# A two-layer graph kernel on one core: no product for the padded key, moments from every fourth row tile, U1's projections in more banks, spare transposes at the start

## The chip, the core and the metric

The kernel runs on one core of one Trainium2 chip. The metric is the device time of one execution in microseconds (us). The kernel before took 2207.8 us (median of three runs, 2207.56 to 2210.33).

## What is computed

`x` is 3327 x 256, `adj` is 3327 x 3327, sparse with its diagonal set, all float32. Two layers follow each other, each on a layer norm and relu of `x`, and each result is added to `x`. Cut to what matters here:

```python
# layer 0, on h = relu(layernorm(x))
R = (adj + eye) / rowsum(adj + eye)
Z, Xf, Xa = 0, h, h
for n in range(2):
    q, k = Xa @ W1.T @ W2.T, Xa @ W3.T          # 64 wide
    probs = softmax(q @ k.T)                    # 3327 x 3327
    A = probs with each row cut to its top entries summing to 0.9, renormalised
    Xf, Xa = R @ Xf, A @ Xa
    Z = Z + Xf @ U1[n].T + Xa @ U2[n].T
x = x + layernorm(h + Z) * ln_g + ln_b

# layer 1: 4-head neighbour attention on relu(layernorm(x)), then elu, added to x
```

## The kernel before, in words

**Tiles.** The 3327 rows are 26 tiles of 128; the last has 127 real rows, so tile arrays are one column longer (3328) than the real data. Work goes row tile by row tile, twice (two steps), and then through the neighbour attention of layer 1.

**Stages.** (1) The start: 26 loads of `x` (L1830 in `load_x`), mean and deviation on VectorE and GpSimd (`deviations`), relu on ScalarE (L1169), two transposes per tile on TensorE (L1174) copied to `c` (L1177), then one product per tile with the combined weights `wqk` that gives keys and queries together (L1182), copied to a ring of three `kq` buffers (L1188) and spread from there by GpSimd (L1191, L1192) and a DMA (L1195). (2) `project_u`: each tile of `h` times both U1 matrices (two products of 128 x 512, L1218). Half of the result goes to `main` by ScalarE (L1221), the other half to `c` by VectorE (L1222). (3) Two steps of 26 rows each. A row's `search` makes its logits in two parts (L882, into two `pl` tiles of two banks each), exponentials (L896), counts over the whole row at two or three guessed thresholds (L933), candidate windows on VectorE (L988, L993), a sort and choice, and four pieces that zero what falls below the threshold (L1043). `attention` then transposes the row (26 transposes, L1056) and multiplies (26 products of 128 x 256, L1068, in the bank `acca`). `full` multiplies a row tile of `adj` with the source (26 products, L1100, in the bank `accf`). (4) Neighbour attention in four blocks (L1644, L1660, L1674).

**The padded key.** Logits for the last 255 keys come in two halves of 128 and 127 columns, one from each half of the 128 partitions. For the 3328th column, which is no key, a product of two constant tiles `none` (L890) writes -1000 into the logits, so that its exponential is 0.

**The moments.** The first threshold is guessed from mean and variance of each row's logits, which follow from the sum of the keys and of their outer products. `moments` takes them from a sample of key tiles: a transpose of the tile's `kq` (L771), a copy to one of two `kk` buffers (L775), a product of 128 x 65 (L780), and additions to `gk` (L792). `keys_summed` puts it for every second tile, 13 per step, in step 0 in the banks `acca` and `accf`, in step 1 in `px`. `stats` (L807 and after) makes the rows' figures of it.

**What sets the order.** The order is made when the program is built: `Plan` (class at L470) is a planner that runs at build time. Every piece of work is put with an engine, an assumed length, a rank, its needs, and the buffers that it takes and gives back. The planner walks through the assumed time, gives each free engine the ready piece with the lowest rank, and writes the instructions in that order. On the chip each engine works through its own list in that order and waits where an operand or a buffer is not ready. The buffers in PSUM are `pl` (two of two banks each), `acca` and `accf` (one bank each) and `px` (two of one bank each). In the start `px` serves the key products, U1's projections and the statistics.

`project_u` is planned at rank -1.9 (TensorE), its copies at -2.6, a row's logits and exponentials at 2.5 below the row's number.

Of the kernel before, what the change touches and what calls it, by code (L numbers as in the profile page):

```python
# [469 lines left out]
class Plan:  # L470
# [26 lines left out]
    def order(self):  # L497
        free, events = dict(self.free), []
        now = dict.fromkeys(self.LAG, 0.0)
        ready = {e: [] for e in self.LAG}  # L500

        def finish(p, end):

            heapq.heappush(events, (end, p["k"], p, "own"))
            heapq.heappush(events, (end + p["lag"], p["k"], p, ""))
            for b in p["give"]:
                heapq.heappush(events, (end + p["lag"], p["k"], p, b))

        for k, p in enumerate(self.pieces):
            p["k"], p["left"], p["from"] = k, len(p["needs"]), 0.0  # L510
            if not p["left"]:
                ready[p["engine"]].append(p)
        out, clock, holds = [], 0.0, []
        while len(out) < len(self.pieces):
            while events and events[0][0] <= clock:
                _, _, p, what = heapq.heappop(events)
                if what == "end":

                    held = sum(max(0.0, min(z, clock) - max(a, p["at"])) for a, z in holds[-12:])
                    end = p["at"] + p["length"] + held  # L520
                    if end > clock + 1e-6:
                        now[p["engine"]] = end
                        heapq.heappush(events, (end, p["k"], p, "end"))
                    else:
                        finish(p, clock)
                    continue
                if what not in ("", "own"):
                    free[what] += 1
                    continue
                for q in p["then"]:  # L530
                    if (q["engine"] == p["engine"]) == (what == "own"):
                        q["left"] -= 1
                        if not q["left"]:
                            ready[q["engine"]].append(q)
            for e, queue in ready.items():
                if now[e] > clock or not queue:
                    continue
                can = [p for p in queue if all(free[b] >= p["take"].count(b) for b in p["take"])]
                if not can:
                    continue  # L540
                p = min(can, key=lambda q: q["rank"])
                queue.remove(p)
                for b in p["take"]:
                    free[b] -= 1
                p["at"] = clock
                now[e] = clock + p["length"]
                if p["hold"]:
                    holds.append((clock, clock + p["hold"]))
                if e == "POOL":
                    heapq.heappush(events, (now[e], p["k"], p, "end"))  # L550
                else:
                    finish(p, now[e])
                out.append(p)
            times = [t for e, t in now.items() if t > clock and ready[e]] + ([events[0][0]] if events else [])
            later = [t for t in times if t > clock]
            if not later:
                if len(out) < len(self.pieces):
                    raise RuntimeError("the plan stands still")
                break
            clock = min(later)  # L560
        self.end = max(now.values())
        return out
# [8 lines left out]
def fast(  # L571
# [59 lines left out]
    with ExitStack() as l0:  # L631
# [16 lines left out]
        kt = wpool.tile([P, 3 * 512 + P], F32, name="kt")  # L648
        qq = wpool.tile([P, NT, P], F32, name="qq")


        none = wpool.tile([P, P + 2], F32, name="none")
        GP.memset(none, 0.0)
        GP.memset(none[DA : DA + 32, :P], 1.0)
        GP.memset(none[DA : DA + 32, P:], -1.0e3)
        kks = [wpool.tile([P, P + 2], F32, name=f"kk{k}") for k in range(2)]
        for kk in kks:
            GP.memset(kk[:, :: P + 1], 1.0)
# [103 lines left out]
        def moments(t, kq, ps_k, ps_g):  # L762


            r, p = side(t), min(P, N - t * P)
            half = slice(r * DA, r * DA + DA)
            held = {}

            def turn():
                held["ps"] = ps_k()  # L770
                T.transpose(held["ps"][:, :P], kq(), ident)  # L771

            def copy():
                kk = held["kk"] = kks[t // 2 % 2]
                S.copy(kk[:, 1 : P + 1], held["ps"][:, :P])  # L775

            def product():
                kk = held["kk"]
                ps = held["ps"] = ps_g()
                T.matmul(  # L780
                    ps[:, : DA + 1], kk[:p, 1 : P + 1], kk[:p, r * (DA + 1) : (r + 1) * (DA + 1)], start=True, stop=True
                )

            def gather():
                for to, src in (
                    (gk[half, :DA], held["ps"][half, 1 - r : DA + 1 - r]),
                    (gk[half, DA : DA + 1], held["ps"][half, DA * r : DA * r + 1]),
                ):
                    if t in (0, 4):
                        V.tensor_copy(to, src)  # L790
                    else:
                        V.tensor_add(to, to, src)  # L792

            return turn, copy, product, gather
# [59 lines left out]
        class Row:  # L854
# [18 lines left out]
            def logits(self, k):  # L873

                if k == 0:
                    self.open()
                pl = ps_l.tile([P, 2, 512], F32, name="pl")
                w = 512 if k < 3 else P
                for r in range(2):
                    m = min(w, N - 1024 * k - w * r)  # L880
                    half = slice(r * DA, r * DA + DA)
                    T.matmul(  # L882
                        pl[:, r, :m],
                        qq[half, self.i, :],
                        kt[half, 512 * k : 512 * k + m],
                        start=True,
                        stop=True,
                    )
                    if m < w:
                        T.matmul(pl[:, r, m:w], none[half, :P], none[half, P : P + w - m], start=True, stop=True)  # L890
                self.pl[k] = pl[:, :, :w]

            def exps(self, k):
                pl = self.pl.pop(k)
                w = pl.shape[2]
                S.activation(  # L896
                    self.e[:, 1024 * k : 1024 * k + 2 * w].rearrange("p (r w) -> p r w", r=2),
                    pl,
                    AF.Exp,
                    accum_out=(self.p0, self.p1, self.p2, self.p3)[k],  # L900
# [94 lines left out]
            def free(self):  # L995

                GP.tensor_scalar(self.room, self.h0, self.h1, self.b, ALU.add, ALU.subtract)
                GP.tensor_scalar(self.rec, self.s, self.h0, self.h1, ALU.subtract, ALU.subtract)

            def sort(self):  # L1000

# [159 lines left out]
        def prepare(t, measured):  # L1161
# [32 lines left out]
            def double():  # L1194
# [7 lines left out]
            a = plan.put("ACT", 0.3, r, share, needs=[a], take=["kq"], give=["px"])  # L1202
            k = plan.put("POOL", 0.7, r, keys, needs=[a])
            q = plan.put("SP", 0.2, r, double, needs=[a])
            g = t % 2 == 0 and keys_summed(
                t, lambda: held["kq"], lambda: ps_a.tile([P, P], F32, name="acca"),
                lambda: ps_a.tile([P, DA + 1], F32, name="accf"), r, [a], ("acca", "accf"), [],
            ) or None
# [3 lines left out]
        def project_u(t, rank):  # L1212
            held = {}

            def product():
                ps = held["ps"] = ps_x.tile([P, 2 * D], F32, name="px")
                for k in range(2):
                    T.matmul(ps, c[:, t, k * P : (k + 1) * P], u1[:, k, :], start=(k == 0), stop=(k == 1))  # L1218

            a = plan.put("PE", 1.75, rank, product, needs=[turned_h[t], uloads], take=["px"])  # L1220
            b = plan.put("ACT", 0.37, -2.6, lambda: S.copy(main[:, t, :D], held["ps"][:, :D]), needs=[a])  # L1221
            e = plan.put("DVE", 0.43, -2.6, lambda: V.tensor_copy(c[:, t, :], held["ps"][:, D:]), needs=[a])  # L1222
            plan.put("SP", 0.0, -2.6, lambda: None, needs=[b, e], give=["px"], lag=0.0)
            return b, e

        def finish1(row, done, rank):
# [59 lines left out]
            if direct:  # L1286
# [2 lines left out]
                    plan.put("POOL", 0.4, r, queries, needs=[a, drawn[0]]),  # L1289
                ]  # L1290
            kq.append(plan.put("SP", 0.3, r, spread, needs=[a, drawn[0] if direct else None]))
            g = t % 2 == 0 and keys_summed(
                t, lambda: held["kq"], lambda: ps_x.tile([P, P], F32, name="px"),
                lambda: ps_x.tile([P, DA + 1], F32, name="px"), r, [a, guessed[0]], ("px", "px"), [],
            ) or None
# [123 lines left out]
        def search(row, rank, keys, stats_of, fresh):  # L1419
# [4 lines left out]
            for g in range(2):  # L1424

                def logits(g=g):
# [1 line left out]
                    row.logits(2 * g + 1)  # L1428

                a = plan.put(  # L1430
                    "PE", 2.1 - 0.7 * g, rank - 2.5, logits, needs=[keys, fresh, a], take=["pl", "pl"] + ["e", "sc"] * (1 - g)
                )
                for k in (2 * g, 2 * g + 1):
                    got.append(
# [394 lines left out]
        def load_x(t):  # L1829
            nc.sync.dma_start(rhs[0][:, t, :], x[t * P : (t + 1) * P, :])  # L1830

        uloads = []
        weighed = weights()
        loads = [plan.put("SP", 0.58, -200.0 + t, load_x, t) for t in range(NT)]
# [8 lines left out]
        for n in range(STEPS):  # L1843
            base = 30.0 * n
            scaled = plan.put(
                "DVE", 0.2, base - 50.0,
                lambda: V.tensor_scalar(gk[:, : DA + 1], gk[:, : DA + 1], 1.0 / (NT // 2 * P), None, ALU.mult), needs=[sums],
            )
            cuts = (0, 3, NT // 2, NT)
            of = {}  # L1850
# [121 lines left out]
```

## Time and profile before

| What | Value |
|---|---|
| Median of three runs | 2207.8 us |
| The profiled execution | 2208.77 us |
| Its span | 2207.0 us |
| TensorE busy | 2169.5 us, 98% |
| VectorE busy | 1614.3 us, 73% |
| ScalarE busy | 1443.2 us, 65% |
| GpSimd busy | 932.8 us, 42% |
| First instruction of TensorE | 5.96 us |
| First logits (L882) | 46.9 us |
| First transposed row piece (L1056) | 105.1 us |
| Last logits (L882) | 1637 us |

The profile is one execution. "PE" is TensorE's matmuls and "PEld" its weight loads; DVE is VectorE, ACT ScalarE, POOL GpSimd, SP the engine that issues most DMAs. A line of the groups names the source line, the engine, the operation, what is written and read, the shape and the number of records. A float32 product leaves two records of TensorE, a transpose one. [...] records overlap, and the pace is read from the distance of starts. A line of the timeline merges a run of equal instructions: start, length, what, number of records, and in brackets an idle time before it with what ended it.

### The profile page before, as it was taken

The page shows a single profiled execution, that of the slowest core. Times are in us where ns is not written, and L with a number is a line of the kernel's source. Part 1 is how long each engine was busy: PE and PEld are TensorE (multiplying, and loading weights), DVE is VectorE, ACT ScalarE, POOL GpSimd, SP SyncE. Part 2 cuts the span into 40 slices and gives each one's busy share as a digit, 9 for nine tenths or more (in the row PEclk, how much of TensorE's full clock was granted, in tenths as well). Part 3 has the DMA queues.
Part 4 walks back from the last instruction along what each step waited for, and adds up shares of the span by engine and source line. Part 5 has one row for each costly group of instructions (what it writes and reads, how often), then busy time and mean ns, then how long its engine had stood idle before and what let it go on. Part 6 is the DMA issues. An engine that isn't in the chain of part 4 may idle for free. (4 is left out here: it accounts for less than half of the span.)

```text
span 2207.0 us, 35945 instructions
## 1 busy us (share of the span) xinstructions
PE 2169.5 (98%) x11978; PEld 1530.4 (69%) x11978; DVE 1614.3 (73%) x4229; ACT 1443.2 (65%) x2726; POOL 932.8 (42%) x2210
## 2 busy tenths in 40 slices
PE   8999999999999999999999999999999999999997
PEld 6488778778877788878777888878888433333332
DVE  5566757546665573177979798787778997989896
ACT  5776776566666751478787878778764555455553
POOL 5554465435454550255665656666663100000001
PEclk9999999999999999999999999999999999999999
DMA  4012121212212232532212222222224444444341
GB/s 120 1 45 85 49 70 50 75 52 61 73 49 76 65 92 80 185 84 63 67 55 62 60 72 71 77 63 63 71 77 143 137 126 138 116 141 124 110 128 52
DMA packets 192323, 183.75 MB, mean 83 GB/s; under 512 B 15386, under 2 KB 146176, under 8 KB 192128
## 3 DMA queue, kind: packets, MB, share of 16 engines
q1 hardware_dynamic: 191232, 181.15, 28.3%
q8 instruction: 96, 1.57, 0.3%
q14 instruction: 99, 0.81, 0.1%
q10 hardware_dynamic: 896, 0.21, 0.0%
HBM read 164.41 MB, written 15.94 MB: 82 GB/s over the span
## 5 line engine op out<-in xcount | busy, mean ns | idle before, releaser
L1068 PE MATMUL acca<-rhs,et 128*128 128x256 f32 x2704 | 616.8, 379 | 0.0
L933 ACT ACTIVATE junk<-e,sc 128x3327 fp8e5<-128x3327 f32 x182 | 559.0, 3071 | 68.3 <-POOL sc L978 67.6
L1068 PEld LDWEIGHTS acca<-rhs,et 128*128 128x128 f32 x2704 | 499.3, 190 | 62.5 <-issue 1.5
L1100 PE MATMUL accf<-c,at 128*128 128x256 f32 x1352 | 316.8, 383 | 4.7 <-ACT f L1107 4.5
L1100 PE MATMUL accf<-main,at 128*128 128x257 f32 x1352 | 310.9, 381 | 1.0 <-ACT f L1107 0.5
L988 DVE SCALAR_TENSOR_TENSOR y<-e,sc 128x1664 f32<-128x1664 f32 x104 | 208.9, 2009 | 131.6 <-POOL sc L975 129.6
L1100 PEld LDWEIGHTS accf<-c,at 128*128 128x128 f32 x1352 | 248.7, 190 | 51.0 <-issue 10.6
L1100 PEld LDWEIGHTS accf<-main,at 128*128 128x128 f32 x1352 | 250.8, 190 | 46.1 <-issue 9.4
L1061 ACT COPY et<-px 128x512 f32<-128x512 f32 (+1 forms) x364 | 192.3, 553 | 125.0 <-PE px L1056 69.8
L993 DVE MAX8 cands<-y 128x8 f32<-128x208 f32 x832 | 242.2, 361 | 3.6
L1043 DVE SCALAR_TENSOR_TENSOR e<-e,thr 128x832 f32<-128x832 f32 x208 | 213.0, 1079 | 1.8
L896 ACT ACTIVATE e<-pl 128x1024 f32<-128x1024 f32 x208 | 179.8, 868 | 42.0 <-PE pl L882 41.7
L1633 ACT ACTIVATE et<-at 128x448 bf16<-128x448 f32 (+1 forms) x204 | 112.3, 550 | 129.1 <-DVE e L1644 75.8
L1056 PE MATMUL px<-ident,e 128*128 128x128 f32 x1352 | 190.8, 274 | 5.4 <-ACT et L1061 2.5
L1796 POOL TENSOR_TENSOR qq<-qq 128x256 f32<-128x256 f32 x4 | 3.0, 754 | 452.3 <-ACT qq L1792 452.2
L1660 PE MATMUL pl<-e,main 128*64 128x416 f32 x1024 | 191.3, 517 | 0.2
L1056 PEld LDWEIGHTS px<-ident,e 128*128 128x128 f32 x1352 | 159.4, 141 | 45.4 <-issue 13.5
L882 PE MATMUL pl<-kt,qq 64*128 64x512 f32 (+1 forms) x832 | 173.5, 535 | 0.0
L1660 PEld LDWEIGHTS pl<-e,main 128*64 128x64 f32 x1024 | 70.8, 137 | 112.2 <-issue 87.1
L1644 DVE SCALAR_TENSOR_TENSOR e<-c,low,et 128x832 f32<-128x832 f32 x128 | 128.5, 1072 | 8.6 <-PE accf L1674 7.0
L882 PEld LDWEIGHTS pl<-kt,qq 64*128 64x128 f32 x832 | 71.6, 186 | 83.6 <-issue 80.3
L1644 DVE SCALAR_TENSOR_TENSOR e<-qq,low,et 128x832 f32<-128x832 f32 x120 | 120.5, 1075 | 6.0 <-PE accf L1674 4.4
(528 smaller groups left out, 3080.0 us busy)
## 6 DMA issues: line engine op xcount, KB each, us to landing
at<-in_adjt_dram SPq DMA_DIRECT2D x414, 256.0 KB
at<-in_adjt_dram SPq DMA_DIRECT2D x102, 192.0 KB
at<-in_adjt_dram SPq DMA_DIRECT2D x52, 128.0 KB
ys<-ystage SPq DMA_DIRECT2D x26, 256.0 KB
rhs<-in_x_dram SPq DMA_DIRECT2D x26, 128.0 KB
ystage<-in_x_dram SPq DMA_DIRECT2D x26, 128.0 KB
base<-ys SPq DMA_DIRECT2D x26, 128.0 KB
x1s<-ystage SPq DMA_DIRECT2D x26, 128.0 KB
```

The lines of the kernel that those rows point to most:

```text
L882: T.matmul(pl[:, r, :m], qq[half, self.i, :], kt[half, 512 * k : 512 * k + m], start=True, stop=True,)
L896: S.activation(self.e[:, 1024 * k : 1024 * k + 2 * w].rearrange("p (r w) -> p r w", r=2), pl, AF.Exp, accum_out=(self.p0, self.p1, self.p2 ...
L933: S.activation(junk[:, :N], self.e[:, :N], fn, bias=t, scale=-1.0, accum_out=dst, saturate=False)
L988: V.scalar_tensor_tensor(self.y[:, : hi - lo], self.e[:, lo:hi], self.up, self.e[:, lo:hi], ALU.is_lt, ALU.mult, accum_out=(self.h0, self. ...
L993: V.max(self.cands[:, o // PIECE, :], self.y[:, o - lo : min(o + PIECE, hi) - lo])
L1043: V.scalar_tensor_tensor(piece, piece, self.thr[:, o : o + 1], piece, ALU.is_gt, ALU.mult)
L1056: T.transpose(pt[:, k, :], self.e[:, j * P : (j + 1) * P], ident)
L1061: S.copy(self.et[g][:, :m, :], self.pt.pop(g)[:, :m, :])
L1068: T.matmul(self.acc, et[:, j - 4 * g, :], rhs[self.n][:, j, :], start=(j == 0), stop=(j == NT - 1))
L1100: T.matmul(self.acc[:, : self.w], self.at[j // JC][:, j % JC, :], self.src[:, j, : self.w], start=(j == 0), stop=(j == NT - 1),)
L1644: V.scalar_tensor_tensor(held["e"][:, k, :], extra["both"][b % 2][:, k, :], low[:, j, k : k + 1], held["mask"], ALU.max, ALU.mult,)
L1660: T.matmul(q["acc"][a][k * FH : (k + 1) * FH, c, :C], main[:, j, h * FH : (h + 1) * FH], held["e"][:, h, c * C : (c + 1) * C], start=(j == 0),
```

## The change

Six edits, all in the fast path:

- The two halves of a logits tile are written side by side, as one flat range of columns, and the product for the padded key is gone, with its constants. The last exponential covers 255 columns instead of 256. GpSimd sets the padded column of each row's `e` to zero, in `free`.
- `moments` takes every fourth key tile: 7 instead of 13 per step. The divisor follows.
- `project_u` uses `px` only for the first eight tiles; from tile 8 on it uses `acca` for even and `accf` for odd tiles. Its copies are ranked at -2.3 instead of -2.6.
- 34 transposes of the identity into `accf` are put on TensorE at the very end of the ranks (90.0), ready 1.9 us after the planner's start; they hold `accf` until the last of them.
- The planner takes all events that fall due at the present time before it goes on.
- The assumed length of a row's logits is 0.1 shorter for each of the two parts.

```diff
@@ Plan.order
                 out.append(p)
+            if events and events[0][0] <= clock:
+                continue
             times = [t for e, t in now.items() if t > clock and ready[e]] + ([events[0][0]] if events else [])
@@ fast
-        none = wpool.tile([P, P + 2], F32, name="none")
-        GP.memset(none, 0.0)
-        GP.memset(none[DA : DA + 32, :P], 1.0)
-        GP.memset(none[DA : DA + 32, P:], -1.0e3)
@@ moments
-                kk = held["kk"] = kks[t // 2 % 2]
+                kk = held["kk"] = kks[t // 4 % 2]
@@ Row.logits
+                pl = pl.rearrange("p r w -> p (r w)")
                 for r in range(2):
                     m = min(w, N - 1024 * k - w * r)
                     half = slice(r * DA, r * DA + DA)
+                    lo = 512 - w + w * r
                     T.matmul(
-                        pl[:, r, :m],
+                        pl[:, lo : lo + m],
...
-                    if m < w:
-                        T.matmul(pl[:, r, m:w], none[half, :P], none[half, P : P + w - m], start=True, stop=True)
-                self.pl[k] = pl[:, :, :w]
+                self.pl[k] = pl[:, 512 - w : lo + m]
@@ Row.free
                 GP.tensor_scalar(self.rec, self.s, self.h0, self.h1, ALU.subtract, ALU.subtract)
+
+                GP.memset(self.e[:, N:], 0.0)
@@ prepare and finish1
-            g = t % 2 == 0 and keys_summed(
+            g = t % 4 == 0 and keys_summed(
@@ project_u
+            bank = ("acca", "accf")[t % 2] if t > 7 else "px"
+
             def product():
-                ps = held["ps"] = ps_x.tile([P, 2 * D], F32, name="px")
+                ps = held["ps"] = (ps_x if bank == "px" else ps_a).tile([P, 2 * D], F32, name=bank)
...
-            b = plan.put("ACT", 0.37, -2.6, lambda: S.copy(main[:, t, :D], held["ps"][:, :D]), needs=[a])
-            e = plan.put("DVE", 0.43, -2.6, lambda: V.tensor_copy(c[:, t, :], held["ps"][:, D:]), needs=[a])
+            b = plan.put("ACT", 0.37, -2.3, lambda: S.copy(main[:, t, :D], held["ps"][:, :D]), needs=[a])
+            e = plan.put("DVE", 0.43, -2.3, lambda: V.tensor_copy(c[:, t, :], held["ps"][:, D:]), needs=[a])
@@ search
-                    "PE", 2.1 - 0.7 * g, rank - 2.5, logits, ...
+                    "PE", 2.0 - 0.8 * g, rank - 2.5, logits, ...
@@ before the loads of x
+        def idle():
+            if not spare:
+                spare.append(ps_a.tile([P, P], F32, name="accf"))
+            T.transpose(spare[0], ident, ident)
+
+        spare = []
+        a = plan.put("SP", 0.02, -202.0, lambda: None, lag=1.9)
+        for k in range(34):
+            a = plan.put("PE", 0.21, 90.0, idle, needs=[a], take=["accf"] * (k == 0), give=["accf"] * (k == 33), lag=0.0)
@@ the scale of the moments
-                lambda: V.tensor_scalar(gk[:, : DA + 1], gk[:, : DA + 1], 1.0 / (NT // 2 * P), None, ALU.mult), needs=[sums],
+                lambda: V.tensor_scalar(gk[:, : DA + 1], gk[:, : DA + 1], 1.0 / (-(-NT // 4) * P), None, ALU.mult), needs=[sums],
```

In the list of TensorE as it is built with the change, 19 of the 34 transposes stand ahead of the first tile's transposes and the rest between the next ones. Nine tiles of U1's projections stand ahead of the first logits (two before). Ahead of the first transposed row piece stand all 26 U1 tiles in both, the same six parts of logits, 22 of the statistics' 26 products (13 before), and 16 products of the first row of `full` (none before).

More of the change, by code (lines that the diff above doesn't have):

```diff
@@ L888, in logits @@
                     )
-                    if m < w:
-                        T.matmul(pl[:, r, m:w], none[half, :P], none[half, P : P + w - m], start=True, stop=True)
-                self.pl[k] = pl[:, :, :w]
+                self.pl[k] = pl[:, 512 - w : lo + m]
             def exps(self, k):
                 pl = self.pl.pop(k)
-                w = pl.shape[2]
                 S.activation(
-                    self.e[:, 1024 * k : 1024 * k + 2 * w].rearrange("p (r w) -> p r w", r=2),
+                    self.e[:, 1024 * k : 1024 * k + pl.shape[1]],
                     pl,
@@ L1213, in project_u @@
             held = {}
+            bank = ("acca", "accf")[t % 2] if t > 7 else "px"
             def product():
-                ps = held["ps"] = ps_x.tile([P, 2 * D], F32, name="px")
+                ps = held["ps"] = (ps_x if bank == "px" else ps_a).tile([P, 2 * D], F32, name=bank)
                 for k in range(2):
                     T.matmul(ps, c[:, t, k * P : (k + 1) * P], u1[:, k, :], start=(k == 0), stop=(k == 1))
-            a = plan.put("PE", 1.75, rank, product, needs=[turned_h[t], uloads], take=["px"])
-            b = plan.put("ACT", 0.37, -2.6, lambda: S.copy(main[:, t, :D], held["ps"][:, :D]), needs=[a])
-            e = plan.put("DVE", 0.43, -2.6, lambda: V.tensor_copy(c[:, t, :], held["ps"][:, D:]), needs=[a])
-            plan.put("SP", 0.0, -2.6, lambda: None, needs=[b, e], give=["px"], lag=0.0)
+            a = plan.put("PE", 1.75, rank, product, needs=[turned_h[t], uloads], take=[bank])
+            b = plan.put("ACT", 0.37, -2.3, lambda: S.copy(main[:, t, :D], held["ps"][:, :D]), needs=[a])
+            e = plan.put("DVE", 0.43, -2.3, lambda: V.tensor_copy(c[:, t, :], held["ps"][:, D:]), needs=[a])
+            plan.put("SP", 0.0, -2.6, lambda: None, needs=[b, e], give=[bank], lag=0.0)
             return b, e
@@ L1291, in finish1 @@
             kq.append(plan.put("SP", 0.3, r, spread, needs=[a, drawn[0] if direct else None]))
-            g = t % 2 == 0 and keys_summed(
+            g = t % 4 == 0 and keys_summed(
                 t, lambda: held["kq"], lambda: ps_x.tile([P, P], F32, name="px"),
@@ L1430, in search @@
                 a = plan.put(
-                    "PE", 2.1 - 0.7 * g, rank - 2.5, logits, needs=[keys, fresh, a], take=["pl", "pl"] + ["e", "sc"] * (1 - g)
+                    "PE", 2.0 - 0.8 * g, rank - 2.5, logits, needs=[keys, fresh, a], take=["pl", "pl"] + ["e", "sc"] * (1 - g)
                 )
```

## The prediction

> **What bounds the kernel.** I read the page first, for the busy share of each engine.
>
> ```profile
> span 2207.0 us, 35945 instructions
> ...
> PE 2169.5 (98%) x11978; PEld 1530.4 (69%) x11978; DVE 1614.3 (73%) x4229; ACT 1443.2 (65%) x2726; POOL 932.8 (42%) x2210
> ```
>
> TensorE has work in 98% of the span, so work taken from it counts in full wherever it is not waiting. A stage can still wait, so I read TensorE's timeline. At the start a key product's records are 8 in 1.91 us; a little later 8 in 1.25 us:
>
> ```profile
> 16.00 1.91 PE L1182 MATMUL px<-c,wqk 128*128 128x128 f32 x8
> ...
> 21.85 1.25 PE L1182 MATMUL px<-c,wqk 128*128 128x128 f32 x8
> ```
>
> The distance of starts halves from 0.213 to 0.109 us between 17.7 and 18.2 us: up to there the array ran at half pace. Next, the same timeline from the first logits to the first transposed row piece:
>
> ```profile
> 61.17 9.11 PE L1218 MATMUL px<-late,c 128*128 128x512 f32 x20 [1.84 <-ACT main L1221]
> ...
> 72.57 7.13 PE L1218 MATMUL px<-late,c 128*128 128x512 f32 x16 [0.90 <-ACT main L1221]
> ...
> 86.82 3.70 PE L1218 MATMUL px<-late,c 128*128 128x512 f32 x8 [1.57 <-ACT main L1221]
> ...
> 98.16 7.13 PE L1218 MATMUL px<-late,c 128*128 128x512 f32 x16 [0.21 <-ACT main L1221]
> 105.13 0.60 PE L1056 MATMUL px<-ident,e 128*128 128x128 f32 x4
> ```
>
> U1's projections (L1218) stand between the search of row 0 and its attention, and stop where ScalarE, inside a 3 us count, has not emptied `px`; with one stop of 0.41 on VectorE the gaps are 4.9 us. From 105 us on the table of stretches shows TensorE idle for about 11 us up to 1700 us: the rows are at its limit.
>
> [...] continuous work starts at 12.3 us and the pace changes 5.4 us later. [...]
>
> **The padded key.** One row's second logits part, then what follows; and a part without the extra product, in the same timeline:
>
> ```profile
> 1566.15 1.99 PE L882 MATMUL pl<-kt,qq 64*128 64x512 f32 x8
> 1568.07 1.13 PE L1100 MATMUL accf<-c,at 128*128 128x256 f32 x4
> ...
> 1571.97 1.35 PE L882 MATMUL pl<-kt,qq 64*128 64x512 f32 x8
> 1573.16 0.28 PE L890 MATMUL pl<-none 64*128 64x1 f32 x2
> 1573.37 0.92 PE L1100 MATMUL accf<-c,at 128*128 128x256 f32 x3
> ```
>
> The first part takes 1.92 us: four pairs at 0.43 (the two halves of the partitions run side by side) and a seam of 0.2. The second takes 1.40; two pairs at 0.43, two at 0.107 and the same seam would be 1.27. So the product costs 0.13 us although its records say 0.2. All 52 lie on TensorE's path: 52 x 0.13 = **6.8 us** (ends 0.11, one short pair, and 0.21, up to the next start: 5.7 to 10.9). What replaces it is a [128 x 1] zeroing on GpSimd; the row for such a one at the very start is 0.10 us. It stands behind the two instructions that the choice waits for, ahead of other GpSimd work of the next row, on an engine 42% busy; I cost it nothing, at worst 52 x 0.1 if GpSimd's steps were the bound. The transposes read the column some 10 us later.
>
> **The moments.** One of them among a row's work:
>
> ```profile
> 133.76 0.27 PE L771 MATMUL px<-ident,kq 128*128 128x128 f32 x1
> 133.87 1.03 PE L1100 MATMUL accf<-main,at 128*128 128x257 f32 x4
> 134.74 0.33 PE L780 MATMUL px<-kk 128*128 128x65 f32 x2
> 134.91 0.61 PE L1056 MATMUL px<-ident,e 128*128 128x128 f32 x4
> ```
>
> By the starts, 0.11 + 0.17 = 0.28 us. Twelve fewer: **3.4 us**. Their copies and additions on ScalarE and VectorE are off the path.
>
> **The start, up to the first transposed piece at 105.13 us.** I count TensorE's work there at full pace: 52 transposes at 0.109 (5.7), 26 key products at 0.43 (11.2), 13 moments (3.6), 26 U1 tiles at 1.72 (44.8), six logits parts (8.4), three padded products (0.4), 13 statistics products at 0.217 (2.8), the weights (0.6): 77.5 us. So 27.6 us are lost. Split: to the first key product at 13.23 us, 11.3 (waits for `x` and `wqk`); to the first logits at 46.94, 7.8 (33.7 less 25.9), of which 2.2 is the half clock from 13.2 to 17.7 and the rest waits on the three `kq` buffers; to 105.13, 8.5 (58.2 less 49.7), 4.9 of it the gaps above and 3.6 seams.
>
> With the change: the 11.3 stays, since `wqk` comes from ScalarE at 12.85. The spares cost 19 x 0.213 = 4.0 us from 1.9 us on, ending where the first tile is ready at 5.96; the other 15 (1.6 to 3.2 us) fall into gaps there. The half clock is the unknown: 0 if the spares raise it, 2.2 [...]; I take the middle, 1.1. The 5.6 us of `kq` waits now lie beside seven more U1 tiles (12 us of work without `px`); I keep 2.5. The 4.9 us go, four buffers in place of two; the seams stay, and 1.0 is added, as `full` (now 16 products ahead of the first piece) starts its loads after U1's last copy. Lost: 11.3 + 1.1 + 2.5 + 3.6 + 1.0 = 19.5, a gain of **8.1 us** (ends 2 and 13). What is late next is row 0's search: its first piece was ready at 95.5, 48.6 us after its first logits. With the change TensorE has 49.4 us of work in between, so it just fits.
>
> The copies' new rank puts them behind row 0's exponentials and ahead of the counts; only U1 waits for that.
>
> **The new order.** Between a row's last logits and its first transpose TensorE had, for rows 0 to 3, 45, 49, 58 and 65 us of work; in the changed order 44, 43, 48 and 59; later rows are alike. A search took 43 us there (52.6 to 95.5). I take 2 us for waits in rows 1 and 2 (0 to 8). The planner's other edits only reshuffle; bounds -2 to +3, value 0.
>
> Sum: 6.8 + 3.4 + 8.1 - 2.0 = 16.3. The profiled execution took 2208.8 (span 2207.0), so 2192.5; the median of the runs shown is 1.0 lower, so **2191.5 us**.
>
> **The rivals.** *The spares do not do what they are put for* [...]: the clock stays low to 17.7 us and cold spares delay tiles, 1.1 + 1.5 more: 2194. [...] against it, nothing measured. *Row 0's search sets the start* because its logits come later behind U1 tiles: of the 8.1 nothing is left, 2199.6. For it, the fit within 1 us; against it, 16 products of `full` as filler. *Slower: the searches of rows 0 to 2 become the bound.* TensorE's list is fixed, so it stands at a row's first transpose until its pieces are cut. If three searches at once on ScalarE (counts of 3.07 us each) stretch one to 56 us, the cover of 44, 43 and 48 (47, 46 and 51 with seams) is short by 9 + 10 + 5 = 24 us, in place of the 2 us that I took: 2191.5 - 2 + 24 = 2213.5. It decides from about 55 us. Against it: row 0 took 43 us while U1's copies and row 1 shared its engines. *The gains are eaten*: rows' gain partly turned into waits, 2204 to 2212. The fallback to the slow general path, if a thinner sample misses a row's window, would add over 1000 us (L1068 and L1100 alone are 1244 us busy, and it repeats their products); worked through on the inputs, the chosen entries stay within the windows for both samples.
>
> **Chances.** Forecast (2185 to 2197) 0.60; clock 0.13; row 0 0.14 (a seventh of it beyond 2203); gains eaten 0.07; searches 0.05; fallback 0.01. The bounds of the unknown costs run from 2182 to 2203; 2185 to 2201 leaves out about two in ten. A change below 0.2% (4.4 us) cannot be told from none here. Faster 0.85, same 0.09, slower 0.06.
>
> **What would show it.** No L890, and second parts 1.27 us long (right) or still 1.4; 14 L771 records; the pace of 0.109 us before or after 13 us; no gap ahead of U1's products; the first transposed piece at about 102 us with 16 L1100 products done; no wait on L1043 at rows 1 and 2. A first piece after 108 us, or idle TensorE at rows 1 to 3, would make the prediction wrong; a gain above 25 us would mean that more than the start was waiting.

## The result, and the profile after

The changed kernel takes **2197.0 us** (median of five runs, 2193.86 to 2197.6), the kernel before in the same session 2208.8 us (five runs, 2207.56 to 2210.33). The medians are 11.8 us apart, about 0.5%; the ratio of the runs is 0.9943, with a 95% interval of 0.9932 to 0.9954, so the kernel is faster. The profiled execution of the changed kernel is the 2193.86 us one, 3.1 us below its own median; the profiled execution of the kernel before lies at its median. So the two traces differ by 14.9 us and the medians by 11.8, and a part of the study is about that difference.

The page of the kernel after: the span, and busy time, share and records by engine.

```profile
span 2192.1 us, 35711 instructions
...
PE 2158.7 (98%) x11872; PEld 1519.1 (69%) x11872; DVE 1605.3 (73%) x4205; ACT 1441.6 (66%) x2714; POOL 926.6 (42%) x2259
```

TensorE's busy time falls by 10.8 us, although 34 transposes were added, and its share stays 98%. Now TensorE's timeline of the kernel after at the start (start, length, what, records; in brackets the idle time before and what ended it):

```profile
1.78 3.94 PE L1838 MATMUL accf<-ident 128*128 128x128 f32 x19 [1.78 <-POOL ident masks.py:199]
...
6.13 0.71 PE L1838 MATMUL accf<-ident 128*128 128x128 f32 x5
...
13.11 1.92 PE L1181 MATMUL px<-c,wqk 128*128 128x128 f32 x8
...
15.67 1.06 PE L1181 MATMUL px<-c,wqk 128*128 128x128 f32 x8
...
19.91 0.44 PE L1173 MATMUL pl<-ident,rhs 128*128 128x128 f32 x2 [2.51 <-ACT rhs L1168]
```

The spare transposes (L1838) run at about 0.2 us each, and from 6.1 us on at 0.11: the pace does go up behind them. But tiles arrive slowly from 8 to 12 us, and at 13.11 the key products are back at half pace, 8 records in 1.92 us, as before the change. At 17.4 TensorE waits 2.5 us for tile 8. It is not the load of `x` that is late. VectorE has its part of the deviations of tiles 8 to 10 ready at 14.33 us, but GpSimd, which finishes them (L1147), has three pairs of copies of `kq` ahead of that in its list, as the timelines of the two engines show:

```profile
14.15 0.18 DVE L1143 BATCH_NORM_AGGREGATE mvs<-bst 128x2 f32<-128x6 f32 x1
...
17.02 0.29 POOL L1191 COPY qq<-kq 64x128 f32<-64x128 f32 x1
17.40 0.23 POOL L1147 TENSOR_SCALAR mvs<-mvs 128x3 f32<-128x3 f32 x1
```

In the kernel before, the same step begins at 14.60 us, so this wait comes with the new order. The stretch from the first logits to the first transposed piece:

```profile
70.21 5.31 PE L1220 MATMUL px<-late,c 128*128 128x512 f32 x12
...
89.45 1.98 PE L1220 MATMUL accf<-late,c 128*128 128x512 f32 x4 [0.23 <-DVE c L1224]
...
95.40 7.12 PE L1099 MATMUL accf<-main,at 128*128 128x257 f32 x32
...
103.35 1.50 PE L882 MATMUL pl<-kt,qq 64*128 64x512 f32 x8 [0.83 <-ACT e L893]
104.78 1.09 PE L1055 MATMUL px<-ident,e 128*128 128x128 f32 x8
```

Ahead of U1's products (L1220) only 0.23 us of idle time is left of 4.9, and 16 products of `full` (32 records) come before the first piece at 104.78 us. In the second step there is a wait that the kernel before did not have:

```profile
1559.68 3.62 PE L1099 MATMUL accf<-c,at 128*128 128x256 f32 x16
1566.53 1.09 PE L1055 MATMUL px<-ident,e 128*128 128x128 f32 x8 [3.23 <-ACT et L1060]
1567.46 1.03 PE L1099 MATMUL accf<-c,at 128*128 128x256 f32 x4
```

ScalarE's own timeline in the same kernel says why:

```profile
1562.85 3.07 ACT L930 ACTIVATE junk<-e,sc 128x3327 fp8e5<-128x3327 f32 x1 [5.39 <-POOL sc L975]
1565.82 0.19 ACT L930 ACTIVATION_READ_ACCUMULATOR junk<-e,sc 128x1 f32 x1
1565.91 0.56 ACT L1060 COPY et<-px 128x512 f32<-128x512 f32 x1
```

The copy that would free `px` (L1060) could have run at 1559.9. It stands in ScalarE's list behind another row's count (L930), which waits 5.39 us for a threshold from GpSimd. All that lies behind in the list waits too, and with it TensorE.

Where the time went, by the starts of the same row's work in both traces: at the first logits of step 1 (26 rows done) the kernel after is 14.3 us ahead, at the end of the rows 13.6, at the end of the span 14.9. So in these two executions all of the gain comes up to the end of step 0, and step 1 adds nothing.

### The profile page after: what moved, and what is told of

It is laid out like the page before. It is cut to its first block, busy times and chain, and to the rows that moved or that the text cites. A ratio compares the mean times of both kernels' runs of the same rounds, so it can differ in the third digit from the quotient of the medians.

```text
span 2192.1 us, 35711 instructions
## 1 busy us (share of the span) xinstructions
PE 2158.7 (98%) x11872; PEld 1519.1 (69%) x11872; DVE 1605.3 (73%) x4205; ACT 1441.6 (66%) x2714; POOL 926.6 (42%) x2259
## 3 DMA queue, kind: packets, MB, share of 16 engines
q8 instruction: 95, 1.56, 0.3%
## 5 line engine op out<-in xcount | busy, mean ns | idle before, releaser
L930 ACT ACTIVATE junk<-e,sc 128x3327 fp8e5<-128x3327 f32 x182 | 558.8, 3070 | 81.4 <-POOL sc L975 81.0
L1060 ACT COPY et<-px 128x512 f32<-128x512 f32 (+1 forms) x364 | 192.6, 553 | 119.5 <-PE acca L1067 62.9
```

What stands on the lines that cost most here:

```text
L930: S.activation(junk[:, :N], self.e[:, :N], fn, bias=t, scale=-1.0, accum_out=dst, saturate=False)
L1060: S.copy(self.et[g][:, :m, :], self.pt.pop(g)[:, :m, :])
```

## The experiments

The theory after the result: the gain is the sum of the banks, the moments and the padded product, each about as forecast. The rivals: the spares are what shortens the start; the missing part of the forecast went into new waits; or into TensorE's clock. The kernel before took 2208.8 to 2209.4 us in the sessions; a saving is the difference to the median of its session.

**1. The changed kernel once more.** No edit.

> The changed kernel once more. Theory: about 2197 us again, with single runs between 2194 and 2198; a second profile, beside the first one's 2193.9, shows in which stage executions of the same program differ (the start with its clock, or the waits of the rows). Rival: the spread is noise over the whole span, and no stage holds it.

2197.11 us (2196.14 to 2198.33), ratio 0.9944 (0.993 to 0.9957). The gain stands, and its profiled execution is one at the median. It shows what an ordinary execution has that the first profile did not. TensorE's timeline, at 20 us and at the wait of step 1:

```profile
18.55 0.44 PE L1173 MATMUL pl<-ident,rhs 128*128 128x128 f32 x2 [2.58 <-ACT rhs L1168]
20.65 1.23 PE L1181 MATMUL px<-c,wqk 128*128 128x128 f32 x4 [1.65 <-ACT kq L1187]
...
1569.35 1.85 PE L1055 MATMUL px<-ident,e 128*128 128x128 f32 x8 [3.28 <-ACT et L1060]
1571.00 1.91 PE L1099 MATMUL accf<-c,at 128*128 128x256 f32 x4
```

Behind the same wait eight transposes take 1.85 us, not 1.09, and four records of `full` 1.91, not 1.03: TensorE falls to half pace. At the start it stays there until 26.7 us, and the first logits come at 54.67 instead of 51.79 us. From there to 1535 us the two executions are a constant 2.6 to 2.9 us apart; at 1569 another 0.9 is added (3.6 in all; the span is 3.2 longer). The instructions are the same ones.

**2. No spare transposes**, the order kept.

```diff
-            if not spare:
-                spare.append(ps_a.tile([P, P], F32, name="accf"))
-            T.transpose(spare[0], ident, ident)
+            pass
```

> The changed kernel with the same written order, but none of the 34 spare transposes issued. Theory: the trace of the change shows the pace at 0.11 us by 5.9 us, but back at 0.21 us from 11.9 to 15 us, after a gap; so the spares are worth little: within 1 us of the changed kernel. Rival A (the clock matters for the start): 2 to 4 us slower. Rival B (the spares hold up the first tiles): 1 to 2 us faster.

2197.04 us (2194.87 to 2198.08), ratio 0.9942 (0.9929 to 0.9956): the spares are worth nothing that can be measured. TensorE's timeline of this kernel:

```profile
5.93 0.69 PE L1173 MATMUL pl<-ident,rhs 128*128 128x128 f32 x2 [5.93 <-ACT rhs L1168]
...
13.25 1.91 PE L1181 MATMUL px<-c,wqk 128*128 128x128 f32 x8
...
15.74 1.06 PE L1181 MATMUL px<-c,wqk 128*128 128x128 f32 x8
...
19.99 0.44 PE L1173 MATMUL pl<-ident,rhs 128*128 128x128 f32 x2 [2.52 <-ACT rhs L1168]
```

The first tile's transposes take 0.69 us at half pace (0.44 with the spares), but the key products are at 0.213 us each and then at 0.11 in both of these executions, and both stand until 20 us for tile 8. (In the execution of run 1 the key products at 12.8 us already take 0.11 us each, and its first logits are later all the same.) The first logits come at 51.84 us, against 51.79. What the spares win at 6 us is waited away by 20.

**3. The padded product left out alone**, in the kernel before, in place.

```diff
-                if m < w:
-                    T.matmul(pl[:, r, m:w], none[half, :P], none[half, P : P + w - m], start=True, stop=True)
+                GP.memset(self.e[:, N:], 0.0)      # in free
```

(and the flat logits of the change).

> The kernel before with the padded key's product left out alone (flat logits, zeroing on GpSimd), all else and the written order as before. Theory: 52 x 0.13 = 6.8 us less, 2202 us. Rival (the product lies in a seam that stays): under 2 us less, 2207 us.

2208.2 us (2206.11 to 2209.37, 13 runs), ratio 0.9993 (0.9984 to 1.0001): 1.2 us, hardly told from nothing, where 6.8 was forecast. The local price was right. TensorE's timeline in this kernel:

```profile
1572.66 1.35 PE L880 MATMUL pl<-kt,qq 64*128 64x512 f32 x8
1573.94 1.99 PE L1096 MATMUL accf<-c,at 128*128 128x256 f32 x8
```

The part takes 1.28 us now (forecast 1.27). In the first step the rows run 0.12 us earlier one after the other. But in the second step only 1.1 of 3.1 us arrive, and in the profiled execution three falls of the pace eat the rest, by 1.2 us at the start, 1.5 at 62 us and 1.7 at 440 us. The last of them, in the same kernel:

```profile
440.11 0.63 PE L1052 MATMUL px<-ident,e 128*128 128x128 f32 x4 [2.26 <-DVE gk L788]
440.57 2.84 PE L1064 MATMUL acca<-rhs,et 128*128 128x256 f32 x8
443.21 1.81 PE L1052 MATMUL px<-ident,e 128*128 128x128 f32 x8
```

Eight records of L1064 in 2.84 us, where they take 1.89 at full pace.

**4. Seven moments per step alone**, in the kernel before; the order is kept, a left-out moment issues nothing.

```diff
+            if t % 4:
+                return (lambda: None,) * 4
```

> The kernel before with the moments from every fourth tile alone, the written order as before: 12 transposes and 12 products less on TensorE, with their copies and additions. Theory: 12 x 0.28 = 3.4 us less if the start is as bound by TensorE as the rows, 1.7 us less if the start is not: 2205.4 to 2207.1 us. Rival (those products filled waits): no difference.

2206.19 us (2204.55 to 2207.3, 21 runs), ratio 0.9983 (0.9976 to 0.9989): 3.2 us, and 3.4 was forecast. The size agrees, the reason doesn't. In the two traces the first logits come at 46.94 us with all moments and at 47.17 without six of them, so those six gave nothing: both kernels stand until 21.2 or 21.3 us for the same copy of `kq` (what the missing moments leave free lengthens the wait, 2.43 against 0.50 us), and behind the longer wait the pace falls to half until about 26 us, which takes what the later ones save. Of the six in the rows of step 0 about three gave 0.3 us each. And 2.65 us came at one place, in TensorE's timeline of the kernel before:

```profile
434.54 1.90 PE L1100 MATMUL accf<-main,at 128*128 128x257 f32 x8
438.58 0.63 PE L1056 MATMUL px<-ident,e 128*128 128x128 f32 x4 [2.14 <-DVE gk L792]
```

and of the kernel with fewer moments:

```profile
434.22 1.90 PE L1102 MATMUL accf<-main,at 128*128 128x257 f32 x8
435.96 0.60 PE L1058 MATMUL px<-ident,e 128*128 128x128 f32 x4
```

A moment's product held one of the two `px` until VectorE, deep in its own list, had added it. That wait was in no sum of the prediction.

**5. Both of these**, in the kernel before, in place.

> The kernel before with the padded product left out and the moments from every fourth tile, each in place, the order otherwise kept. If the two add up as each alone (1.2 and 3.2 us): 2204.4. If the padded product's saving is held back only where waits for the same bank absorb it, and the missing moments take one of these waits away: 2202 to 2203. If both shorten the way to the same wait: 2205 to 2206.

2202.8 us (2202.27 to 2203.98, 7 runs), ratio 0.9971 (0.9959 to 0.9982): 6.4 us, more than 1.2 + 3.2. At the end of the rows it is 6.9 us ahead of the kernel before and 3.6 ahead of the one with fewer moments alone, so here the padded product gives 3.6 of 6.2 us. The difference to its 1.2 alone fits the falls of the pace: the 2.26 us wait at 440 us is gone with the moments, and the 1.96 us wait at 61 us is not followed by half pace here (only the one at 21 us is). In the second step 1.2 of 3.1 us arrive again.

**6. The padded product put back into the changed kernel**, in place.

> The changed kernel with the padded key's product put back in its written order (and the zeroing on GpSimd taken out). My prediction's term: 52 x 0.13 = 6.8 us slower than the changed kernel's 2197. Theory now: the 0.12 us per row are real, but in step 1 TensorE waits on the row's search as long as it is early, so only step 0's 26 rows and a third of step 1's count: about 4 us slower, 2201. Rival: nothing, as the first trial of leaving it out alone gained only 1.2 us.

2201.48 us is the median of six executions (2200.44 to 2203.53), ratio 0.9969 (0.9957 to 0.998): about 4.5 us are lost. A seventh took 9032.87 us. The mean granted clock of that one is recorded as 0.54, which can't by itself make it four times as long; no trace shows it and its cause stays open. Rows fall behind by 0.12 us each, and about half of that is made up in waits.

**7. U1 in `px` alone**, in the changed kernel, the order planned anew.

```diff
-            bank = ("acca", "accf")[t % 2] if t > 7 else "px"
+            bank = "px"
```

> The changed kernel with U1's projections all in the two px buffers, planned anew. Theory: the waits on ScalarE ahead of U1's products come back in the trace, 5 to 8 us slower: 2202 to 2205. Rival (row 0's search bounds the start in any case): under 2 us slower.

2202.11 us (2199.92 to 2203.97), ratio 0.997 (0.9958 to 0.9981): 5.1 us are lost. The gaps ahead of U1's products are back in this kernel's timeline:

```profile
64.38 9.00 PE L1220 MATMUL px<-late,c 128*128 128x512 f32 x20 [1.97 <-ACT main L1223]
...
89.95 7.32 PE L1220 MATMUL px<-late,c 128*128 128x512 f32 x16 [1.59 <-DVE c L1224]
```

**8. The banks and the copies' rank alone**, in the kernel before, the order planned anew.

```diff
+            bank = ("acca", "accf")[t % 2] if t > 7 else "px"
...
-            b = plan.put("ACT", 0.37, -2.6, lambda: S.copy(main[:, t, :D], held["ps"][:, :D]), needs=[a])
+            b = plan.put("ACT", 0.37, -2.3, lambda: S.copy(main[:, t, :D], held["ps"][:, :D]), needs=[a])
```

> The kernel before with the banks of U1's projections and the rank of their copies alone, planned anew. Theory: waits ahead of U1's products gone, 5 to 8 us faster than before: 2201 to 2204. Rival: the gain needs the other edits (fewer moments in the same banks): under 2 us.

2203.2 us (2202.44 to 2205.37, 12 runs), ratio 0.9976 (0.9968 to 0.9984): 5.6 us. Alone or undone, the banks are the largest part. In this trace TensorE has no wait over 1.2 us between 14 and 1720 us; the one at 438 us is gone with the new order as well, so this part and the moments overlap and the parts need not add up. The profiled execution is the slowest of the twelve: its pace is at half from 29.4 to 36.2 us, though no single wait ahead of that is longer than 1.13 us. As the order was planned anew in this run and in run 7, both show the banks together with the order that they bring.

**9. The planner's edit undone**, in the changed kernel.

```diff
-            if events and events[0][0] <= clock:
-                continue
```

> The changed kernel without the planner's edit (events that are due are taken before the next pick); all the rest stays, and the order is planned anew. The banks, the moments and the padded product have given 10.0 of the 12 us one by one. If the planner's edit gives the other 2 by itself, this takes 2199. If the edit only keeps the new due times usable and is worth nothing by itself, 2196 to 2198. If the banks need it, up to 2202, as with the banks undone.

2197.57 us (2196.87 to 2198.0), ratio 0.9946 (0.9933 to 0.996): no difference that can be told, as the value 0 of the prediction had it. The shorter assumed length of the logits was not tried alone.

**10. Cover for the start's waits.** Into the changed kernel, 20 spare transposes ahead of the transposes of tile 8 and 10 behind them, where TensorE waited for tile 8.

```diff
+                for k in range(20 if t == 8 else 0):
+                    T.transpose(held["pt"][:, 1, :P], ident, ident)
```

> The changed kernel with 30 more spare transposes where TensorE waits longest at the start (20 ahead of tile 8's transposes, 10 after them). Theory: executions of one program differ by 2.9 us because TensorE's pace falls to half after the waits of 2.5 and 1.7 us between 16 and 20.7 us; with these filled it does not: 2194, with runs closer together. Rival A (the spares hold up the queue): 1 to 3 us slower than the changed kernel. Rival B (the pace has another cause): 2197 as it is.

2196.16 us (2194.29 to 2198.08), ratio 0.9944 (0.9931 to 0.9957): not told from the changed kernel. In the trace the start no longer falls (first logits at 52.45 us), but the wait of step 1 does, 3.25 us and then eight transposes in 1.97.

**11. Cover for the wait of step 1 too**: 28 more in row 21, into its free accumulator.

```diff
+                if (self.n, self.i, g) == (1, 21, 1):
+                    fill = ps_a.tile([P, P], F32, name="acca")
+                    for k in range(28):
+                        T.transpose(fill, ident, ident)
```

> The changed kernel with the 30 spare transposes of the start's two waits, and 28 more in the wait near 1563 us (row 21 of step 1, ahead of its second group of transposed pieces, into the row's free accumulator bank). The rows' work is unchanged. If TensorE's fall to half pace behind a wait of 2 us and more is the cost (2.9 us in the first and 1.8 to 2.9 in the second), neither wait can start it any more: the eight transposes behind the wait take 1.0 to 1.1 us and not 1.9 to 2.0, and the median is 2193.5, 2.5 to 3.5 below the changed kernel's 2197.0. If the half pace is set by something else than the idle time ahead of it, it stays and the median is 2196 to 2197. If the fill delays the pieces by itself (28 x 0.11 = 3.1 us in a wait of 3.2), 2197 or more.

2195.21 us (2194.66 to 2196.68), ratio 0.9938 (0.9924 to 0.9952). TensorE's timeline of this kernel:

```profile
18.68 0.44 PE L1179 MATMUL pl<-ident,rhs 128*128 128x128 f32 x2 [0.40 <-ACT rhs L1172]
18.95 1.25 PE L1181 MATMUL pl<-ident 128*128 128x128 f32 x10
21.08 0.71 PE L1189 MATMUL px<-c,wqk 128*128 128x128 f32 x4 [0.87 <-ACT kq L1195]
...
1563.46 3.22 PE L1055 MATMUL acca<-ident 128*128 128x128 f32 x28
1566.83 1.09 PE L1059 MATMUL px<-ident,e 128*128 128x128 f32 x8 [0.15 <-ACT et L1064]
1567.76 1.03 PE L1103 MATMUL accf<-c,at 128*128 128x256 f32 x4
```

The time that the copy takes to come is the same, but the work behind it runs at full pace. In its profiled execution no row is more than 0.7 us behind the fastest execution of the changed kernel. The gain was forecast as 3.5 us and is 1.8 to 1.9, and the intervals of the ratios overlap; but four of its five executions took 2194.66 to 2195.38 us, while of ten of the changed kernel one took 2193.86 and nine 2196.01 to 2198.33. By its median it is the fastest kernel here. Why it isn't 2193.5 is open: executions other than the profiled ones leave only a mean granted clock (0.997 or 0.998 here), which is too coarse to tell.

## Why the prediction was right, and where it was not

The forecast was 2191.5 us, within 2185 to 2201; it took 2197.0. Faster was right, and the likeliest case (2185 to 2197) was met at its very edge. The missing 5.5 us are three terms: 1.4 in the profiled execution (2193.86 against 2192.5), 1.0 of the step to the median (the kernel before's own median came out at its profiled execution), and 3.1 by which an ordinary execution of the new kernel is above its profiled one.

- **The start** was sized well: 20.6 us of TensorE's time lost up to the first piece, by the prediction's own count, where 19.5 were forecast and 27.6 were lost before. Split as there: 11.2 to the first key product (11.3), 5.8 to the first logits (1.1 + 2.5), 3.6 after them (4.6). The banks did what they were costed for. The 2.5 us kept for the waits on `kq` are right by size alone: up to the first logits TensorE's waits on `kq` fell from 1.2 to 0.3 us, and the wait of 2.5 us for tile 8, which the new order makes on GpSimd, came in their place. The work beside these waits was miscounted: in the kernel before, four tiles of U1's projections stand ahead of the first logits, not two, so with the change it is five more and not seven (8.6 us of work, not 12). The half clock went with something that the prediction did not count, the idle time ahead of it: with the spares it ends at 5.2 us in the profiled execution, it is back from 12.0 to 15.4, behind 1.55 us of idle time in the 3.41 us ahead of that, and in run 2, without spares, it ends at 15.4 too. That it lasted to 18.2 us in the kernel before was no property of that kernel: in runs 3 and 5, which have its start and no spares, it ends at 14.7 and 14.8. The first piece came at 104.8 us, not at about 102, since about 2 us more work was planned ahead of it than reckoned (nine more products of the statistics at 0.217), and 1.1 more was lost.
- **The spares** were the first rival: that with them the clock stays low to 17.7 us, which no trace of the kernel before had shown. It did not: behind a run of float32 transposes alone the pace went from 0.2 to 0.11 us within 4.3 us (1.78 to 6.13), and the first tile's pair took 0.44 us, where it took 0.69 in run 2, without spares. The rival's outcome, that the spares give nothing, held for another reason, the wait for tile 8 up to 20 us.
- **The padded product** is the step that failed: "All 52 lie on TensorE's path". The price of 0.13 us was right and arrives row by row in the first step. In the second, some 2 of the 3.1 us are handed back: in three pairs of traces with the same order (the kernel before and run 3; runs 4 and 5; runs 6 and 1) 1.1 to 1.3 us arrive. TensorE's waits from 870 us to the end of the rows (total us, how often, the longest), in run 6, with the product:

```profile
PE accf L1101 <- ACT f L1108: 5.9, 10, 1.2
PE px L1057 <- ACT et L1062: 3.2, 1, 3.2
PE px L1057 <- DVE e L1044: 0.2, 1, 0.2
```

and in the changed kernel, without it:

```profile
PE accf L1099 <- ACT f L1106: 5.7, 10, 1.1
PE px L1055 <- ACT et L1060: 3.5, 2, 3.2
PE px L1055 <- DVE e L1042: 1.1, 3, 0.6
PE accf L1099 <- DMA at<-in_adjt_dram: 0.6, 1, 0.6
```

  9.3 us of waits became 10.9, 1.6 more; in the other two pairs it is 8.0 to 9.2 and 7.9 to 9.5. The prediction's first view had said that TensorE has work in 98% of the span; the step took that for a bound of every row. Most of these waits end on a copy by ScalarE. The rival of eaten gains (0.07) named this, but for the whole change.
- **The moments** came to the forecast amount (3.2 of 3.4), but by a chance: at least half of the twelve saved nothing, and one wait of 2.14 us that a moment caused, costed nowhere, made up for them.
- **The new order** was costed at 2.0 us of waits in rows 1 and 2. There are none on the pieces; the search wasn't stretched, and the rival that ended on the slow side did not come. Instead the order made the 3.2 us wait in row 21 of the second step (it is in run 6 too, so it is not the padded product's), which the prediction's sums of the rows' cover could not show, and the wait for tile 8 at the start.
- **The unpriced cost**: the prediction priced each wait by its length. Behind some idle times TensorE also runs at half pace, which cost 0.9 to 2.9 us more where it was measured.

## What to carry to other kernels

A share of 98% says that the engine is nearly always busy, not that any work taken from it shortens the span: take a saving repeated per row only as far as the row's next wait, and look at which wait grows. A buffer held by a low-ranked step of another engine can cost more than the step, as one moment's `px` did (a wait of 2.14 us, for a moment of 0.28). And before a small gain is put down to an edit, profile two executions of the same program and compare the granted clock: here they differ by 3.2 us, with identical instructions.

## What the runs showed of the hardware

**Half pace behind idle time, as these traces have it.** A trace holds the clock that TensorE was granted. In the fastest execution of the changed kernel it changes at 5.19, 12.02, 15.43 and 2182.89 us, so 6.83, 3.41 and 2167.46 us apart: 2, 1 and 635 times 3.413. In the kernel before it changes at 18.20 and 2199.32 us, 639 times 3.413 apart, and in run 1 the two falls end at 26.7 and 1572.93 us, 453 times. So in each of these three executions the changes lie on a grid of 3.413 us, and its first point differs: 1.78 us from the start of the span in the first, 1.13 in the second, 2.80 in the third. The stretch at half pace from 12.02 us and run 1's from 1569.52 last 3.41 us, that of run 8 from 29.4 us lasts 6.8. What followed a wait went with how it fell on the grid. Two pairs of stretches show it, around the same wait of row 21. A line gives start and end, length, TensorE's busy time, records, granted clock, and the share and rate of DMA. First the fastest execution of the changed kernel:

```profile
1561.67:1565.08 3.41, 1.63 (x8) 1.00 0.55 154
1565.08:1568.50 3.42, 1.97 (x14) 1.00 0.02 5
```

and run 1, the same program:

```profile
1566.10:1569.51 3.41, 0.16 (x1) 1.00 0.27 77
1569.52:1572.93 3.41, 3.41 (x14) 0.50 0.03 7
```

The wait of 3.23 us is split over two stretches there, and the clock stays full. Here nearly all of the wait of 3.28 us lies in one stretch, and the next one runs at half pace. All stretches of such a grid at full pace, up to 2150 us, in the 13 profiled executions:

| Idle time of TensorE in one stretch | half pace in the next one | full pace kept |
|---|---|---|
| 2.16 to 3.25 us | 11: runs 1 (two), 3 (two), 5, 6, 7 (two), 9 (two), 10 | none |
| 1.52 to 1.98 us | 7: profiled run of the changed kernel, runs 3, 4, 6 (two), 8, 9 | 8: kernel before (two), profiled run of the changed kernel, runs 2, 3, 4, 5, 7 |
| up to 1.48 us | none | all others |

The numbers are those of the experiments. So less than a whole idle stretch was enough here (1.55 us in the one from 8.60 to 12.02 us of the changed kernel), and several short waits did it together: in run 8 none of those in the stretch from 26.0 to 29.4 us is longer than 1.13 us, and half pace followed their 1.56 us. What decides between 1.52 and 1.98 us is open: in the kernel before 1.84 us, in the stretch from 59.16 to 62.57, was followed by full pace. Where a fall was measured between two executions or against a neighbour, it cost 0.9 to 2.9 us. Where runs 10 and 11 put transposes of the identity into the waits, no stretch there had more than 1.1 us of idle time, and the pace stayed, in all three places.

**Full pace behind float32 transposes alone**, 0.11 us each where the first took 0.2, as above. With the spares the granted clock is full from 5.19 us in the fastest execution of the changed kernel, and the pace is full by 6.0 us in run 9 and by 6.4 in run 11; up to then TensorE has done nothing but transposes. Without them full pace comes at 18.2 us in the kernel before, at 15.4 in run 2, and at 14.7 and 14.8 in runs 3 and 5.
